# Last pass of a graph-attention and expert kernel: scalings three groups ahead, experts' pieces at the end of a step, and two late additions moved into the pass

## The chip, the cores and the metric

The kernel runs on one core of a Trainium2 chip. The metric is the device time of one execution in microseconds. Engines are named as in the profile: PE (TensorE), DVE (VectorE), ACT (ScalarE), POOL (GpSimd) and SP (SyncE, which here issues nearly all plain transfers). Each engine works through its own instructions in the order of the program.

## The reference

Input are 12500 nodes with 256 features and 212500 directed edges (self-loops included), sorted by target. First a graph attention layer with 4 heads adds its result to the nodes. Then a mixture of experts is applied to the new nodes x1. Cut to what matters here:

```python
x1 = x + gnn(layernorm(x))                       # attention over edges, bias, layernorm, relu
xn = layernorm(x1)
logits = mean(xn over all nodes) @ Wr + br       # ONE routing for all nodes
w, e = the two largest of the routing weights    # softmax of the two
y_k = gelu(xn @ W1[e_k] + b1[e_k]) @ W2[e_k] + b2[e_k]       # k = 0, 1
out = x1 + layernorm(w_0*y_0 + w_1*y_1 + xn, gamma, beta)
```

The routing needs the mean over all nodes, so it is known only when the last node has been through the attention layer. The last layernorm is taken over the feature axis of each node.

## The kernel before

**Tiles and groups.** The nodes are cut into 98 tiles of 128 rows (the last has 84), and the tiles into 25 groups of four (the last group, 24, has two tiles). The path of the code that these inputs take is `by_tiles` and then `weighted_sums`.

**The long loop** of `by_tiles` (L921 to L948) goes through 196 units of edges: POOL gathers rows, DVE and ACT make weights and messages, PE sums them for each tile. When a group's tiles are summed, a generator `nodes` (L398) is started for it. Each turn of the loop advances every running generator by one `yield`. `nodes` ends with three things: the statistics of x1 go to `stat` and PE adds the group's part of the mean to `pm` (L458); x1 is stored (L462); and one `yield` later DVE adds the vector beta to x1 (`xb`, L466), and that is stored as `x1b` (L469). The tile `xb` is in a pool with one buffer.

**The guess.** After group 0 the kernel guesses the two experts. It then runs the experts of a group in the shadow of the long loop (`experts`, L834): load xe, scale it on ACT (L841), transpose on PE (L850), copy (L855), eight hidden products with Gelu on ACT (L863, L868), and for each of the two experts two output products (L882), which DVE adds up (L886) and SP stores in `both` (L888). Between these are 12 `yield`s. The groups that are not begun by the end of the loop, the last three in the profile, are left to a generator `others` (L971), which starts a new chain each seven calls.

**After the loop** (L950 to L969) SP issues the loads of the first seven groups of the last pass (`final_loads`: two pieces of `both` and one of `x1b`, 512 KB each). The generators that still run are those of groups 23 and 24; they are driven to their end. Then the parts of the mean are added up (`sm`, L965), and `route` finds the real experts and their weights `ewc`. If the guess was right, the last pass follows.

**The last pass**, `weighted_sums` (L1290), goes through the 25 groups, one to a step. For each group it holds three slots out of seven of each kind: u and v (the results of the two experts, with the features on the partitions) and xb. For the first 16 groups (`MIXED`) ACT scales u by the first weight (L1306), DVE forms v times the second weight plus u (L1307), and PE transposes the result into PSUM (L1322). For the other groups PE does the weighing itself by two products with a weighted identity (L1325). DVE takes the statistics (L212, L213), ACT the root (L219), DVE the reciprocal and the offset (L220, L1339), ACT normalises in four instructions (L1343), and `stored` multiplies by gamma (L1352) and adds xb (L1354) into u's slot, which SP stores as output (L1356). The loads of group i + 7 into the slots of group i are issued last in step i. The tiles of PSUM are taken in turn from five buffers, two for a group.

The order within a step is written out by hand, and it is the order on each engine:

```python
        for i in range(NG):
            normed(i)
            weighed(i + 2)
            next(others, None)
            statistics(i + 1)
            transposed(i + 2)
            if i % 2:
                next(others, None)
            stored(i)
            held[i + SLOTS] = final_loads(take, i + SLOTS)
```

Of the kernel before, what the change touches and what calls it, by code (L numbers as in the profile page):

```python
# [37 lines left out]
F32 = mybir.dt.float32  # L38
# [8 lines left out]
P = 128  # L47
GN = 4
# [6 lines left out]
TOP_K = 2  # L55
# [4 lines left out]
def gnn_ffn_kernel(ctx: ExitStack, tc: tile.TileContext, x, src, dst, W, att_src, att_dst, bias,  # L60
                   g_gamma, g_beta, Wr, br, W1, b1, W2, b2, f_gamma, f_beta, out):
    nc = tc.nc
# [15 lines left out]
    def rows(t):  # L78
        return min(P, N - t * P)
# [318 lines left out]
    def nodes(pool, pm, a0, xc, ts, parts=((0, NT),), pool1=None):  # L398

        t0 = ts[0]
        den = pool.tile([P, GN, H], F32, name="den")
        for r, c0, c1 in spans(ts):
            av = a0[:r, c0:c1, :].rearrange("p t (h c) -> p t h c", h=H)
            nc.vector.tensor_scalar(den[:r, c0:c1, :], av[:, :, :, C], 1e-16, None, op0=ALU.add)
            nc.vector.reciprocal(den[:r, c0:c1, :], den[:r, c0:c1, :])
        yield
        o = (pool1 or pool).tile([P, GN, D], F32, name="o")
        ob = (pool1 or pool).tile([P, GN, D], F32, name="ob")  # L410
        for r, c0, c1 in spans(ts):
            n = c1 - c0
            av = a0[:r, c0:c1, :].rearrange("p t (h c) -> p t h c", h=H)
            nc.vector.tensor_tensor(
                o[:r, c0:c1, :].rearrange("p t (h c) -> p t h c", h=H), av[:, :, :, :C],
                den[:r, c0:c1, :, None].to_broadcast([r, n, H, C]), ALU.mult)
            nc.vector.tensor_add(ob[:r, c0:c1, :], o[:r, c0:c1, :],
                                 vec["bias"][:r, None, :].to_broadcast([r, n, D]))
        yield
        mv = pool.tile([P, GN, 2], F32, name="mvc")  # L420
        moments(pool, mv, ts, lambda j, r: ob[:r, j, :])
        yield
        rstd = pool.tile([P, GN], F32, name="rstdc")
        off = pool.tile([P, GN], F32, name="offc")
        inverse_std(pool, rstd, mv, ts)
        for r, c0, c1 in spans(ts):
            nc.vector.scalar_tensor_tensor(off[:r, c0:c1], mv[:r, c0:c1, 0], -1.0,
                                           rstd[:r, c0:c1], op0=ALU.mult, op1=ALU.mult)
        for j, t in enumerate(ts):
            r = rows(t)  # L430
            nc.scalar.activation(o[:r, j, :], ob[:r, j, :], AF.Identity, bias=off[:r, j:j + 1],
                                 scale=rstd[:r, j:j + 1])
        yield
        for r, c0, c1 in spans(ts):
            n = c1 - c0
            nc.vector.tensor_mul(ob[:r, c0:c1, :], o[:r, c0:c1, :],
                                 vec["gg"][:r, None, :].to_broadcast([r, n, D]))
            nc.vector.tensor_add(o[:r, c0:c1, :], ob[:r, c0:c1, :],
                                 vec["gb"][:r, None, :].to_broadcast([r, n, D]))
        yield  # L440
        mv2 = pool.tile([P, GN, 2], F32, name="mv2")
        for r, c0, c1 in spans(ts):
            nc.vector.scalar_tensor_tensor(  # L443
                xc[:r, c0:c1, :D], o[:r, c0:c1, :], 0.0, xc[:r, c0:c1, :D],
                op0=ALU.max, op1=ALU.add)
        moments(pool, mv2, ts, lambda j, r: xc[:r, j, :D])
        yield
        rstd2 = pool.tile([P, GN], F32, name="rstd2")
        inverse_std(pool, rstd2, mv2, ts)
        for r, c0, c1 in spans(ts):  # L450
            nc.vector.tensor_copy(stat[:r, t0 + c0:t0 + c1, 0], mv2[:r, c0:c1, 0])
            nc.vector.tensor_copy(stat[:r, t0 + c0:t0 + c1, 1], rstd2[:r, c0:c1])
            nc.vector.tensor_copy(xc[:r, c0:c1, D], mv2[:r, c0:c1, 0])
            nc.vector.scalar_tensor_tensor(stat[:r, t0 + c0:t0 + c1, 2], mv2[:r, c0:c1, 0], -1.0,  # L454
                                           rstd2[:r, c0:c1], op0=ALU.mult, op1=ALU.mult)
        for j, t in enumerate(ts):
            r = rows(t)
            nc.tensor.matmul(pm[-1], stat[:r, t, 1:2], xc[:r, j, :],  # L458
                             start=any(t == a for a, _ in parts),
                             stop=any(t == b - 1 for _, b in parts))  # L460
        for r, c0, c1, a in node_rows(x1, ts, D):
            nc.sync.dma_start(a, xc[:r, c0:c1, :D])  # L462
        yield
        xb = (pool1 or pool).tile([P, GN, D], F32, name="xb")
        for r, c0, c1 in spans(ts):
            nc.vector.tensor_add(xb[:r, c0:c1, :], xc[:r, c0:c1, :D],  # L466
                                 vec["fb"][:r, None, :].to_broadcast([r, c1 - c0, D]))
        for r, c0, c1, a in node_rows(x1b, ts, D):
            nc.sync.dma_start(a, xb[:r, c0:c1, :])  # L469
# [235 lines left out]
    def by_tiles():  # L705
# [4 lines left out]
        with tc.tile_pool(name="pe", bufs=1) as pe, \  # L710
# [194 lines left out]
            def forward(n):  # L905
# [8 lines left out]
                if (sought is not None and sought not in running and free_at <= n <= U - 12  # L914
# [2 lines left out]
                    running.append(experts(begun))  # L917
                    begun, free_at = begun + 1, n + EG

            waiting = set(range(len(groups)))  # L920
            for n in range(U + 2):  # L921
                if n + AH < U:
                    gather(units[n + AH])
                if n < U:
                    t, k0 = units[n]
                    if k0 == 0 and t % GN == 0:
                        group[t // GN] = node_tiles(pcw, groups[t // GN], table)
                    weights(units[n])
                if n + 1 < U:
                    targets(units[n + 1])  # L930
                if n < U:
                    edge_rows(units[n])
                if n + 2 < U:
                    across_rows(units[n + 2])
                if n < U:
                    messages(units[n])
                if 1 <= n <= U:
                    sums(units[n - 1])
                if n > 1 and units[n - 2][1] + UE >= TE:
                    t = units[n - 2][0]  # L940
                    node_sums(t)
                    g = t // GN
                    if t == groups[g][-1]:
                        a0, xc = group.pop(g)
                        with_nodes[g] = nodes(pcw, pm, a0, xc, groups[g], parts, pco)
                        running.append(with_nodes[g])
                        waiting.discard(g)
                forward(n)  # L948
            assert all(groups[g][0] >= LATE for g in with_nodes)
            sm = pe.tile([1, D + 1], F32, name="sm")  # L950
            nc.vector.tensor_add(sm, sm0, pm[-1])
            of_edges.close()
# [17 lines left out]

            def others():  # L971

                chains, g, n = [], begun, 0
                while chains or g < len(groups):
                    if g < len(groups) and n % EG == 0:
                        chains.append(experts(g))
                        g += 1
                    chains = further(chains)
                    n += 1
                    yield  # L980
# [309 lines left out]
    def weighted_sums(pe, take, psm, ahead, others):  # L1290
# [6 lines left out]
        for k in range(TOP_K):  # L1297
            nc.vector.tensor_scalar(by[:, k, :], ident, ewc[:, 2 * TOP_K + k:2 * TOP_K + k + 1],
                                    None, op0=ALU.mult)

        def weighed(i):

            if i < MIXED:
                n = sum(rows(t) for t in groups[i])
                u, v = (wide(piece)[:, :, :n] for piece in held[i][:2])
                nc.scalar.mul(u, u, ewc[:, 2 * TOP_K:2 * TOP_K + 1])  # L1306
                nc.vector.scalar_tensor_tensor(v, v, ewc[:, 2 * TOP_K + 1:], u,  # L1307
                                               op0=ALU.mult, op1=ALU.add)

# [36 lines left out]
        def stored(i):  # L1346
            s, _, xb = held.pop(i)
            p = ps.pop(i)
            for r, c0, c1 in spans(groups[i]):
                for c in range(c0, c1, 2):  # L1350
                    e = min(c + 2, c1)
                    nc.vector.tensor_mul(s[:r, c:e, :], p[c // 2][:r, c % 2:c % 2 + e - c, :],  # L1352
                                         vec["fg"][:r, None, :].to_broadcast([r, e - c, D]))
                nc.vector.tensor_add(s[:r, c0:c1, :], s[:r, c0:c1, :], xb[:r, c0:c1, :])  # L1354
            for r, c0, c1, a in node_rows(out, groups[i], D):
                nc.sync.dma_start(a, s[:r, c0:c1, :])  # L1356

        weighed(0)
        transposed(0)
        weighed(1)  # L1360
# [1 line left out]
        transposed(1)  # L1362
        for i in range(NG):
            normed(i)
            weighed(i + 2)
            next(others, None)
            statistics(i + 1)
            transposed(i + 2)
            if i % 2:
                next(others, None)  # L1370
            stored(i)
            held[i + SLOTS] = final_loads(take, i + SLOTS)


    ordered = nc.values_load(in_order, min_val=0, max_val=1)
    with tc.If(ordered != 0) as cmp:
# [31 lines left out]
```

## Time and profile before

| | |
|---|---|
| time, median of 3 runs | 2691.14 us (2683.43 to 2692.22) |
| the profiled execution: time, span | 2687.61 us, 2685.8 us |
| busy share of PE, DVE, ACT, POOL | 75%, 62%, 29%, 65% |
| last gather on POOL, and first step of the last pass (first L1343) | about 2407 us, 2475.35 us |
| last instruction of DVE in the last pass | ends at 2681.1 us |
| transfers over the whole span | 471.26 MB, mean 175 GB/s |

The shares are means over stages with quite different limits. In the last tenth POOL is at rest, so the last pass is read from its own stretch, 2411 to 2685.8 us.

### The profile page before, as it was taken

How to read it: one execution, taken by the hardware profiler on the slowest of the kernel's cores; microseconds unless marked ns; L12 is line 12 of the kernel's file. 1: busy time of each engine (PE TensorE's matmuls, PEld its weight loads, DVE VectorE, ACT ScalarE, POOL GpSimd, SP SyncE). 2: the span in 40 equal slices, each digit the busy share in tenths (PEclk: the TensorE clock that was granted, in tenths of full speed). 3: DMA queues.
4: the chain of work that ended last, by engine and by line, in shares of the span. 5: the costliest groups of instructions: out<-in, count | busy, mean ns of one | idle time of the engine just before them, and what ended most of it. 6: DMA issues, size and time to landing. Idle time of an engine off the chain costs nothing.

```text
span 2685.8 us, 25556 instructions
## 1 busy us (share of the span) xinstructions
PE 2004.4 (75%) x8326; PEld 1299.8 (48%) x8326; DVE 1670.0 (62%) x3149; ACT 788.5 (29%) x1283; POOL 1735.1 (65%) x1835
## 2 busy tenths in 40 slices
PE   6945555687878788878887788778778878872676
PEld 5734443454545555545554454455445544541336
DVE  7844655666565666566665666566666656665558
ACT  3410010232333223333223322322332233222554
POOL 1057777777777777777777777777777777760000
PEclk9977777899989999998889898988998888895788
DMA  7655456555655655665556556556555655545667
GB/s 208 211 162 151 131 165 195 154 171 181 186 144 178 184 175 163 189 180 164 169 179 179 156 180 178 163 158 188 175 161 170 180 179 161 174 123 202 210 216 224
DMA packets 248452, 471.26 MB, mean 175 GB/s; under 512 B 38348, under 2 KB 153800, under 8 KB 248114
## 3 DMA queue, kind: packets, MB, share of 16 engines
q0 software_dynamic: 84928, 240.36, 32.9%
q1 hardware_dynamic: 162566, 228.93, 25.5%
q8 instruction: 67, 1.10, 0.2%
q14 instruction: 75, 0.61, 0.1%
q10 hardware_dynamic: 816, 0.26, 0.0%
HBM read 391.75 MB, written 77.65 MB: 175 GB/s over the span
## 4 chain that ended last, share of the span: by engine, by line
POOL 44%; issue 23%; DVE 16%; DMA 7%; ACT 4%; PE 4%; SPq 1%; ACTq 0%; DVEq 0%; POOLq 0%; another core or an unknown queue 0%
POOL rows_w L729 44%; DMA rows_w<-table,src_c 6%; DVE ms L785 4%; DVE bn L212 3%; DVE oh L779 1%; ACT L772 1%; PE po_w L796 1%; PE ph_e L863 1%; ACT mix L1343 1%; DVE xc L443 1%; DVE whole L1354 1%; DVE ohT L743 1%; DVE whole L1352 1%; DVE y_e L886 1%; PE ph_e L882 1%
## 5 line engine op out<-in xcount | busy, mean ns | idle before, releaser
L729 POOL DMA_INDIRECT rows_w<-table,src_c x1764 | 1720.8, 975 | 539.7 <-issue 520.1
L796 PE MATMUL po_w<-ms,oh 128*128 128x260 f32 x3528 | 945.5, 429 | 2.4 <-DVE ms L785 2.4
L796 PEld LDWEIGHTS po_w<-ms,oh 128*128 128x128 f32 x3528 | 741.9, 215 | 131.8 <-DVE ms L785 3.2
L863 PE MATMUL ph_e<-xT_e,w1s 128*128 128x512 f32 (+1 forms) x800 | 420.5, 663 | 172.1 <-ACT hT_e L868 157.6
L785 DVE TENSOR_TENSOR ms<-rows_w,ad 128x2340 f32<-128x2340 f32 x196 | 506.2, 2583 | 0.0
L766 DVE TENSOR_TENSOR zw<-rows_w,adv 128x36 f32<-128x36 f32 x196 | 38.6, 197 | 637.5 <-DMA rows_w<-table,src_c 554.0
L779 DVE TENSOR_TENSOR oh<-jrow,ad 128x1152 f32<-128x1152 f32 x196 | 265.4, 1354 | 213.8 <-ACT ad L772 207.8
L882 PE MATMUL ph_e<-hT_e,w2s 128*128 128x512 f32 (+1 forms) x800 | 360.9, 595 | 18.3 <-ACT xT_e L855 18.3
L772 ACT ACT_TABLE_LOAD x113 | 145.0, 1283 | 772.5 <-DVE z3w L770 723.7
L863 PEld LDWEIGHTS ph_e<-xT_e,w1s 128*128 128x128 f32 x800 | 159.9, 210 | 365.8 <-ACT hT_e L868 205.9
L754 PE MATMUL ad<-t_all,ohT 128*128 128x25 bf16 x1764 | 77.5, 178 | 282.6 <-DVE ms L785 268.5
L772 ACT ACTIVATE ad<-z3w 128x36 f32<-128x36 f32 x196 | 40.0, 204 | 829.2 <-DVE z3w L770 764.4
L754 PEld LDWEIGHTS <-ohT 128*128 128x128 bf16 x1764 | 66.5, 99 | 404.9 <-DVE ms L785 344.1
L882 PEld LDWEIGHTS ph_e<-hT_e,w2s 128*128 128x128 f32 x800 | 154.0, 195 | 170.2 <-issue 144.2
L868 ACT ACTIVATE hT_e<-ph_e,b1c 128x512 f32<-128x512 f32 (+1 forms) x200 | 124.7, 673 | 13.2 <-PE ph_e L863 12.1
L868 ACT ACT_TABLE_LOAD x97 | 124.5, 1283 | 1.7
L743 DVE TENSOR_SCALAR ohT<-wb,pcol 128x1152 bf16<-128x1152 bf16 x196 | 102.6, 524 | 3.9 <-DMA srow<-in_src_dram,start_i 3.9
L458 PE MATMUL pm<-xc,stat 128*1 128x257 f32 x184 | 61.4, 493 | 51.6 <-DVE stat L454 43.0
L320 PE MATMUL ph<-WE,xT 128*128 128x264 f32 x392 | 96.7, 391 | 0.0
L333 POOL COPY tb<-ad_all 128x16 f32<-128x16 f32 (+2 forms) x26 | 5.1, 198 | 131.8 <-ACT ad_all L328 131.7
L320 PEld LDWEIGHTS ph<-WE,xT 128*128 128x128 f32 x392 | 71.7, 193 | 10.1
L219 ACT ACT_TABLE_LOAD x58 | 74.4, 1283 | 3.4 <-issue 2.4
(206 smaller groups left out, 1449.0 us busy)
## 6 DMA issues: line engine op xcount, KB each, us to landing
wb<-wrow_d SPq DMA_DIRECT2D x98, 576.0 KB
rows_w<-table,src_c POOLq DMA_INDIRECT x1764
both<-y_e SPq DMA_DIRECT2D x48, 512.0 KB
whole<-both SPq DMA_DIRECT2D x48, 512.0 KB
table<-tb SPq DMA_DIRECT2D x24, 528.0 KB
a<-table SPq DMA_DIRECT2D x24, 520.0 KB
xa<-in_x_dram SPq DMA_DIRECT2D x24, 512.0 KB
xc<-in_x_dram SPq DMA_DIRECT2D x24, 512.0 KB
```

Source lines behind the costliest of these rows:

```text
L212: nc.vector.bn_stats(bn[:r, j, :], get(j, r))
L320: nc.tensor.matmul(ph[:r, i, :HC + 2 * H], xT[:, i, d, :r], WE[:, d, :], start=(d == 0), stop=(d == KD - 1))
L729: nc.gpsimd.indirect_dma_start(out=got[u][:, k, :], out_offset=None, in_=table, in_offset=bass.IndirectOffsetOnAxis(ap=src_c[:, k0 + k, t: ...
L743: nc.vector.tensor_scalar(ohT[u], wb[t][:, k0 * P:(k0 + UE) * P], pcol, None, op0=ALU.is_equal)
L754: nc.tensor.matmul(ad[u][:, k * (6 * H + 1):(k + 1) * (6 * H + 1)], ohT[u][:, k * P:(k + 1) * P], t3_all[:, t, :], start=True, stop=True)
L772: nc.scalar.activation(ad[u][:, UW:].rearrange("p (k h) -> p k h", h=H), z3, AF.Exp)
L779: nc.vector.tensor_tensor(oh[u], jrow[:, None, :].to_broadcast([P, UE, P]), av[:, :, 6 * H:].to_broadcast([P, UE, P]), ALU.is_equal)
L785: nc.vector.tensor_tensor(ms[u].rearrange("p t (h c) -> p t h c", h=H), got.pop(u)[:, :, :MW].rearrange("p t (h c) -> p t h c", h=H), w[:, ...
L796: nc.tensor.matmul(po[t], e[:, k, :], m[:, k, :], start=(k0 + k == 0), stop=(k0 + k == TE - 1))
L863: nc.tensor.matmul(ph[m][:, :n], w1s[:, k, d, c * P:(c + 1) * P], xT[:, d, :n], start=(d == 0), stop=(d == KD - 1))
L868: nc.scalar.activation(hT[:, m, :n], ph.pop(m)[:, :n], AF.Gelu, bias=b1c[:, c, k:k + 1])
L882: nc.tensor.matmul(py[:, :n], w2s[:, k, c, d * P:(d + 1) * P], hT[:, k * KF + c, :n], start=(c == 0), stop=(c == KF - 1))
```

## The change

Three things are done. In `nodes`, groups from tile LATE on (the last two, 23 and 24) end after L462, without the addition of beta; the addition is put into a function of its own, `with_beta`, and `others` does it for these two groups at its first call, with two tiles of the pool that has one buffer of each name. In `weighted_sums` the scaling of u by ACT becomes a function of its own, `scaled`, which is called for three groups before the first step and in step i for group i + 3, while DVE's part stays at group i + 2. And the calls of `others` move: the one of each step to its end, behind `stored` and ahead of the loads, and the second one of odd steps from behind the transposes to ahead of them. In the new numbering of the file the lines behind the first edit are shifted.

```diff
@@ nodes
             nc.sync.dma_start(a, xc[:r, c0:c1, :D])
-        yield
-        xb = (pool1 or pool).tile([P, GN, D], F32, name="xb")
+        if t0 < parts[-1][0]:
+            yield
+            with_beta((pool1 or pool).tile([P, GN, D], F32, name="xb"), xc, ts)
+
+    def with_beta(xb, xc, ts):
+
         for r, c0, c1 in spans(ts):
             nc.vector.tensor_add(xb[:r, c0:c1, :], xc[:r, c0:c1, :D],
                                  vec["fb"][:r, None, :].to_broadcast([r, c1 - c0, D]))
@@ by_tiles
+            late = []
...
                         with_nodes[g] = nodes(pcw, pm, a0, xc, groups[g], parts, pco)
+                        if t >= LATE:
+                            late.append((xc, groups[g]))
...
             def others():
 
+                for name, (xc, ts) in zip(("xb", "ob"), late):
+                    with_beta(pco.tile([P, GN, D], F32, name=name), xc, ts)
                 chains, g, n = [], begun, 0
@@ weighted_sums
+        def scaled(i):
+
+            if i < MIXED:
+                n = sum(rows(t) for t in groups[i])
+                u = wide(held[i][0])[:, :, :n]
+                nc.scalar.mul(u, u, ewc[:, 2 * TOP_K:2 * TOP_K + 1])
+
         def weighed(i):
 
             if i < MIXED:
                 n = sum(rows(t) for t in groups[i])
                 u, v = (wide(piece)[:, :, :n] for piece in held[i][:2])
-                nc.scalar.mul(u, u, ewc[:, 2 * TOP_K:2 * TOP_K + 1])
                 nc.vector.scalar_tensor_tensor(v, v, ewc[:, 2 * TOP_K + 1:], u,
                                                op0=ALU.mult, op1=ALU.add)
...
+        for i in range(3):
+            scaled(i)
         weighed(0)
...
         for i in range(NG):
             normed(i)
+            scaled(i + 3)
             weighed(i + 2)
-            next(others, None)
             statistics(i + 1)
-            transposed(i + 2)
             if i % 2:
                 next(others, None)
+            transposed(i + 2)
             stored(i)
+            next(others, None)
             held[i + SLOTS] = final_loads(take, i + SLOTS)
```

More of the change, by code (lines that the diff above doesn't have):

```diff
@@ L948, in by_tiles @@
                 forward(n)
-            assert all(groups[g][0] >= LATE for g in with_nodes)
+            assert [groups[g][0] >= LATE for g in with_nodes] == [True, True]
             sm = pe.tile([1, D + 1], F32, name="sm")
```

## The prediction

> **What bounds the kernel now.** I read the page first (span 2685.8 us, profiled run 2687.61 us), then the chain of waits over the last 270 us, then the timelines of DVE, ACT and SP there, and last the stage windows. Up to about 2411 us the gathers of POOL set the pace and the diff touches nothing in that loop, so all that follows is about 2411 to 2685.8. Three things bound that stretch.
>
> First, the head. The chain, and the same place in the timeline of DVE (start, length, in brackets the idle time before it and who ended it):
>
> ```profile
> 2444.96 1.32 SPq L462
> 2446.38 10.09 DMA x1b<-xb
> 2456.49 0.76 DVE xb L466 x2
> 2458.00 1.02 PE mix L478 x4
> ```
>
> ```profile
> 2437.88 0.15 DVE L454 SCALAR_TENSOR_TENSOR stat<-mv,rstd 84x1 f32<-84x1 f32 x1
> 2456.49 0.76 DVE L466 TENSOR_TENSOR xb<-xc,v_fb 128x256 f32<-128x256 f32 x2 [18.46 <-DMA x1b<-xb]
> 2457.17 0.40 DVE L965 TENSOR_TENSOR sm<-sm,mix 1x257 f32<-1x257 f32 x1
> ```
>
> DVE stands idle for 18.46 us: the xb of the last group has one buffer, which the group before it is still storing, and that store was issued behind 21 loads. The sum for the routing (L965) needs no xb, it only stands behind it in DVE's order.
>
> Second, the steps of the last pass. One quiet step, DVE then ACT, and the two largest rows of the waits from 2457 on:
>
> ```profile
> 2484.58 0.16 DVE L1339 SCALAR_TENSOR_TENSOR offf<-mvf,rstdf 128x4 f32<-128x4 f32 x1
> 2488.06 1.28 DVE L1307 SCALAR_TENSOR_TENSOR whole<-whole,ewc 128x1024 f32<-128x1024 f32 x1 [3.33 <-ACT whole L1306]
> ...
> 2484.83 2.13 ACT L1343 ACTIVATE mix<-mix,offf,rstdf 128x256 f32<-128x256 f32 x4 [2.48 <-DVE offf L1339]
> 2486.89 1.14 ACT L1306 ACTIVATE whole<-whole,ewc 128x1024 f32<-128x1024 f32 x1
> ```
>
> ```profile
> DVE whole L1307 <- ACT whole L1306: 46.7, 15, 3.3
> ACT mix L1343 <- DVE offf L1339: 29.5, 18, 3.1
> ```
>
> DVE waits 3.3 us in each step for a scaling that ACT does only after the four normalisations of another group. A quiet step is 9.5 us (L1343 starts at 2475.35, 2484.83, 2494.32), of which DVE works 6.2.
>
> Third, a bound that hardly shows yet: the turn of SP's queue. The load of group i+7 into the first piece waits until the output of group i, which lies in that slot, has landed, and all that SP issues is in one order.
>
> ```profile
> 2484.52 0.38 SPq L1356 DMA_DIRECT2D out_dram<-whole  x1
> 2487.47 0.88 SPq L1283 DMA_DIRECT2D whole<-both  x2
> ...
> 2646.79 0.88 SPq L1283 DMA_DIRECT2D whole<-both  x2
> 2647.72 0.46 SPq L1162 DMA_DIRECT2D whole<-x1b  x1
> 2648.27 0.68 SPq L1356 DMA_DIRECT2D out_dram<-whole  x1
> 2656.12 0.87 SPq L1283 DMA_DIRECT2D whole<-both  x2
> ```
>
> With the transfers at rest a store holds SP for 2.95 us (2484.52 to 2487.47). Directly behind the three loads it holds it for 7.85, so that one turn (2646.79 to 2656.12) lasts 9.33 us, although the engines move no more than this (last two columns: DMA share, GB/s):
>
> ```profile
> 2425.00:2430.00 5.00, 0.00 (x0) 0.00 (x0) 4.76 (x16) 0.30 (x1) 0.00 (x0) 0.50 1.06 382
> 2646.50:2656.00 9.50, 7.62 (x64) 7.30 (x64) 9.10 (x25) 4.35 (x10) 0.00 (x0) 1.00 0.72 223
> ```
>
> **The change part by part.** *Residual plus beta of the last two groups leaves the nodes.* L466 of group 23 (1.19 us of DVE) and of group 24 (0.76) and three stores of L469 go. L965 then waits only for the four matmuls of L458, which end at 2437.76 + 1.64 = 2439.4; without the 1.19 us ahead of them, and with ACT as the partner in that stretch, I take 0.7 of it: 2438.7. Gain 2457.17 - 2438.7 = 18.5 us. What is late next is the route of 11 us from L965 to ewc, a chain of small DVE steps that I leave as it is; its bounds are 0 and 5 us longer, since it now runs while the loads still fill the transfers (share 1.07 until 2455); DVE's instructions at 2425 to 2437 show no stretching under the same load, so 0.
>
> The two adds come back inside the pass, behind the output of group 0: 1.19 + 0.76 = 2.0 us of DVE, once, and three stores on SP between output 0 and the loads of group 7. SP so waits for the adds and issues four DMAs (with the experts' xe load): the first load, T7, comes 4.0 us after DVE's end of step 0 instead of 3.0.
>
> *Scalings three groups ahead.* The same 16 instructions of L1306 (1.14 each), none added. Three stand ahead of the first step: the third ends some 3.3 us after ewc, while DVE's first two mixes and statistics take until 6 us after it (ACT idled 2.49 us there), so it is hidden. In step 0 the wait of 3.32 for the third mix is gone: DVE ends step 0 at 2484.46 - 18.5 - 3.3 = 2462.7, and T7 = 2466.7.
>
> In quiet steps DVE loses its 3.3: 6.3 us. In steps with an experts' Gelu ACT is the longer one: root 0.30, DVE's two small ones and the hops 0.5, four L1343 2.13, L1306 1.14, table load 1.28, two Gelus 1.26, table load 1.28 = 7.9 us (9.4 before). With two such calls in one odd step 1.26 more and about 1 for the matmul between them: 10 (11.1 before).
>
> *Experts' pieces at the end of a step.* A call issues the same xe loads, ACT, PE and DVE work and stores of both; on PE they now stand behind the transposes, on DVE and ACT behind stored, on SP still ahead of the loads of group i+7, but behind the output. POOL has nothing in the pass. The gain is small (transposes no longer behind 2 to 3 us of experts' matmuls, a delay that L1307's wait covered). The price: an xe load at the end of a step whose scaling stands in the middle of the next one. Before, ACT waited for such a load once (5.2 us, L841). Now that meets steps 1 and 5: about 3 and 8 us, 11 together; behind the waiting L841 on ACT stands the root of the next group, and DVE's reciprocal waits for that.
>
> Engines alone: steps 0 to 13 hold 6 quiet ones (38), 5 with one Gelu call (40), 3 with two (30), plus 11 = 118 us instead of 149.9 (2475.35 to 2625.25): 32 less. From step 14 on DVE takes 4.9 us a step as before.
>
> *The turn.* At 6.3 to 8 us a step DVE is faster than SP's turn of 9.33, so outputs are queued directly behind loads from step 1 on. Here the rule and the row part. The Trainium skill, page "DMA: Bandwidth & Descriptors", section on the anatomy of one DMA, gives about 2.0 us fixed, most of it the receipt of the write, plus the bytes at 436 GB/s. An isolated 512 KB store comes to 3.2 by it and 2.95 by the trace: agreed. For the turn (2.1 MB queued) it gives 2.0 + 4.8 = 6.8 us; then the turn would not bind and the engines' sum stands. The trace has 9.33 and, with the output 1.95 us behind the loads, 8.49 (2627.95 to 2636.44). The measurement decides: I take 9.2, nearer to the state that will hold.
>
> Experts' DMAs lengthen turns: with a 212 KB store of both they were 10.35 and 10.51, so 1.1 each; for 512 KB, scaled by 375 GB/s, 1.9 (an estimate from these rows). Five large ones and three small fall into the 17 turns from T7 to T24: 12.8 us. T24 = 2466.7 + 17 x 9.2 + 12.8 = 2635.9 (2666.63 before). Seven groups of lead let DVE run ahead until about step 21; then statistics of 23 and 24 wait for their loads. From T24: landing 2.7 (as before, 2669.3), 16 matmuls of L1325 1.9, statistics 1.1, output of 23 2.5, from there to the last DVE instruction 3.2, to the span's end 4.7: 16. Span 2652, time 2654 with the 1.8 us around the span. The profiled run was 2687.61, so 34 us less; the median shown, 2691.14, is 3.5 above that run, within the 9 us over which the three runs scatter, so I add nothing.
>
> **The rivals.** *The turn does not bind.* Then the end is 2681.1 - 18.5 - 3.3 - 32 = 2627.3, plus 2.0 for the moved adds and 4.7: span 2634, time 2636. For it: 375 GB/s were reached in the pure loads, and 8.49 was seen. Against: every turn after 2636 is over 9.
>
> *Only the head is gained.* Turns stay at the old mean, 179.2 / 17 = 10.5, because waits of ACT and PE on experts' pieces (15.2 and 15.7 us steps from 2524.28 and 2549.58) return in other places: 2466.7 + 179.2 + 16 = 2662, time 2664; with 5 us in the route and 5 in late xe loads up to 2674.
>
> *Slower.* The mechanism: each experts' DMA stands in SP between an output and the next loads and waits there for a late y_e, so that SP's turn grows until the loads arrive after DVE needs them. It decides when the mean turn passes 12.7 us: 2466.7 + 17 x 12.7 + 16 = 2698.6, time 2700. Turns of 13.0 and 15.3 have occurred (2537.07 to 2565.33), but only there, and a mean of 12.7 would need that in most of the 17.
>
> That the change does not do what it says would be: L965 still waiting for a store. Its inputs are sm and the sum in PSUM only, so I give it no more than the chance of no difference.
>
> **How the numbers follow.** Turn binds, 0.60: 2644 to 2660 (turn 8.7 to 9.7). Engines bind, 0.20: about 2636. Head only, 0.14: 2662 to 2674. No difference, 0.03; slower, 0.03. The time is that of the likeliest, 2654. The range reaches from the second case, with 3 us for scatter, to the top of the third: 2633 to 2674. A measurement of this kernel can tell about 0.3% (8 us) from no change; faster by more than that 0.94, within it 0.03, slower 0.03.
>
> **What would show it.** Right: L965 near 2439 with no long wait ahead of it; the row L1307 waiting for L1306 gone; quiet steps of 6.3 us; SP issuing outputs directly behind loads with turns of about 9 us; late in the pass, DVE's or PE's waits ending in the landing of whole<-both. Wrong: no wait for loads at the end (then 2636 is nearer), or ACT's waits for xe over 15 us in total, or turns above 10.5.

## The result, and the profile after

The changed kernel takes 2656.86 us (median of 4 runs, 2655.96 to 2661.83) against 2691.68 us before (4 runs): ratio 0.988, 95% interval 0.9857 to 0.9904. Its profiled execution has a span of 2654.2 us, 31.6 less than before. Line numbers behind the first edit have moved: L965 is now L972, L1306 is L1315, L1307 is L1322, L1339 is L1354, L1343 is L1358, L1352 is L1367, L1283 is L1292, L1356 is L1371, L841 is L845, L1325 is L1340.

The head, in the timeline of DVE (start, length, what ended the idle time before):

```profile
2437.74 0.14 DVE L454 SCALAR_TENSOR_TENSOR stat<-mv,rstd 84x1 f32<-84x1 f32 x1
2439.54 0.41 DVE L972 TENSOR_TENSOR sm<-sm,mix 1x257 f32<-1x257 f32 x1 [1.65 <-PE mix L458]
```

The wait of 18.46 us for a store is gone. What is left is 1.65 us for PE's last part of the mean; the sum of the means starts 17.6 us earlier than before (2457.17).

A quiet step (one without Gelu of the experts), DVE again:

```profile
2479.76 0.16 DVE L1354 SCALAR_TENSOR_TENSOR offf<-mvf,rstdf 128x4 f32<-128x4 f32 x1
2479.84 1.28 DVE L1322 SCALAR_TENSOR_TENSOR whole<-whole,ewc 128x1024 f32<-128x1024 f32 x1
```

The mix of u and v follows the offset without a gap; before it waited 3.33 us there. The step from L1358 at 2473.95 to that at 2479.96 is 6.0 us, before 9.5.

The queue of SP in the same stretch, and where it ends up:

```profile
2487.74 0.87 SPq L1292 DMA_DIRECT2D whole<-both  x2
2488.66 0.46 SPq L1171 DMA_DIRECT2D whole<-x1b  x1
2489.22 0.50 SPq L1371 DMA_DIRECT2D out_dram<-whole  x1
2496.81 0.87 SPq L1292 DMA_DIRECT2D whole<-both  x2
2497.73 0.46 SPq L1171 DMA_DIRECT2D whole<-x1b  x1
2498.28 0.66 SPq L1371 DMA_DIRECT2D out_dram<-whole  x1
2506.14 0.87 SPq L1292 DMA_DIRECT2D whole<-both  x2
2507.07 0.46 SPq L1171 DMA_DIRECT2D whole<-x1b  x1
2507.58 0.92 SPq L134 DMA_DIRECT2D xe<-x  x1
```

Here an output stands directly behind the loads, and the turn is 9.07 and 9.33 us. Before, such turns came only in the last 60 us; now they come in steps 2 to 5 and again from step 12 to the end. The last four lines also show the new stall: the xe load of the second chain comes behind loads that wait 7.9 us for an output. ACT, for which it was issued, stands still meanwhile, and DVE behind it:

```profile
2515.80 2.07 ACT L845 ACTIVATE xe<-xe,stat 128x256 f32<-128x256 f32 x4 [11.03 <-DMA xe<-x]
...
2519.51 0.18 DVE L220 RECIPROCAL rstdf<-std 128x4 f32<-128x4 f32 x1 [14.11 <-ACT std L219]
```

So in steps 6 to 11 it is SP that waits for DVE: the outputs come 2 to 9 us after SP is free, first here.

```profile
2518.04 0.46 SPq L1171 DMA_DIRECT2D whole<-x1b  x1
2525.73 0.38 SPq L1371 DMA_DIRECT2D out_dram<-whole  x1
```

The end, in the chain of waits:

```profile
2628.49 7.99 DMA out_dram<-whole
2636.53 0.36 SPq L1292
2636.99 2.99 DMA whole<-both
2640.03 2.57 PE mix L1340 x14
2642.62 0.44 DVE bn L212
```

An output holds SP for 8 us, then come the loads of the last group, PE waits for them and DVE for PE. From step 12 on every output is issued right behind its loads, with at most a store of y_e between, so DVE no longer keeps SP waiting: the end is set by the queue of SP. Steps 22 and 23 lose 6.5 us to it (9.5 and 6.4 us where before they took 4.9 and 4.5).

### The profile page after: what moved, and what is told of

Read it like the earlier page. It is cut to its first block, busy times and chain, and to the rows that moved or that the text cites. A ratio compares the mean times of both kernels' runs of the same rounds, so it can differ in the third digit from the quotient of the medians.

```text
span 2654.2 us, 25552 instructions
## 1 busy us (share of the span) xinstructions
PE 2008.5 (76%) x8326; PEld 1303.1 (49%) x8326; DVE 1671.9 (63%) x3149; ACT 788.8 (30%) x1283; POOL 1735.0 (65%) x1835
## 4 chain that ended last, share of the span: by engine, by line
POOL 43%; issue 23%; DVE 17%; DMA 8%; PE 5%; ACT 4%; ACTq 0%; DVEq 0%; SPq 0%; POOLq 0%; another core or an unknown queue 0%
POOL rows_w L733 43%; DMA rows_w<-table,src_c 6%; DVE ms L789 5%; DVE bn L212 2%; PE ph_e L867 2%; DVE oh L783 2%; PE po_w L800 1%; ACT L776 1%; DVE xc L443 1%; DVE ohT L747 1%; DVE y_e L890 1%; DMA out_dram<-whole 1%; PE ph_e L886 1%; DVE mv L213 1%; DVE whole L1367 1%
## 5 line engine op out<-in xcount | busy, mean ns | idle before, releaser
L867 PE MATMUL ph_e<-xT_e,w1s 128*128 128x512 f32 (+1 forms) x800 | 422.7, 666 | 155.4 <-ACT hT_e L872 145.1
L886 PE MATMUL ph_e<-hT_e,w2s 128*128 128x512 f32 (+1 forms) x800 | 354.0, 586 | 13.6 <-ACT xT_e L859 13.0
L867 PEld LDWEIGHTS ph_e<-xT_e,w1s 128*128 128x128 f32 x800 | 162.2, 212 | 349.8 <-ACT hT_e L872 191.5
L886 PEld LDWEIGHTS ph_e<-hT_e,w2s 128*128 128x128 f32 x800 | 151.1, 191 | 161.5 <-issue 139.6
```

The costliest lines, as they stand in the source:

```text
L867: nc.tensor.matmul(ph[m][:, :n], w1s[:, k, d, c * P:(c + 1) * P], xT[:, d, :n], start=(d == 0), stop=(d == KD - 1))
L886: nc.tensor.matmul(py[:, :n], w2s[:, k, c, d * P:(d + 1) * P], hT[:, k * KF + c, :n], start=(c == 0), stop=(c == KF - 1))
```

## The experiments

The theory: with the scalings out of DVE's way, the turn of SP's queue (loads, then an output that has to land before the next loads) sets the end of the pass. The rival: the steps of the engines set it (DVE's work, ACT with its table loads, PE with the experts' matmuls).

Four runs, marked "other chip" below, were on a chip on which the kernel before takes 3325 us (55 runs, granted clock 0.77 in place of 0.88); its long loop is slower there. Two of these kernels were run once more where before takes 2690 us. The pass itself hardly differs: from the start of the sum of the means to the end of the span it took 230.5 and 232.5 us for the one kernel, 216.3 and 217.6 for the other. This stretch, "the pass" from here on, is 228.6 us before and 214.7 after the change. All lengths of passes, steps and turns are of one profiled execution each.

**The head: a buffer, not the additions.** One name is changed in the kernel before; nothing is moved:

```diff
-        xb = (pool1 or pool).tile([P, GN, D], F32, name="xb")
+        xb = (pool1 or pool).tile([P, GN, D], F32, name="ob" if t0 == groups[-1][0] else "xb")
```

> The kernel before with one name changed: the sum with beta of group 24 goes into the tile ob, which is free by then, in place of xb; nothing is moved. Theory: the 18.46 us of DVE are a wait for that one buffer, so the sum of the means starts near 2440 and nearly the whole gain of the head is there: 16 to 18 us faster than before, time about 2673 to 2675. Rival, the additions themselves or their stores are what holds the head: less than 5 us faster.

2671.24 us, ratio 0.9938 (0.9925 to 0.995). Both additions stand where they stood, and DVE has no wait but that for PE:

```profile
2439.28 0.75 DVE L466 TENSOR_TENSOR ob<-xc,v_fb 128x256 f32<-128x256 f32 x2
2441.00 0.41 DVE L965 TENSOR_TENSOR sm<-sm,mix 1x257 f32<-1x257 f32 x1 [0.97 <-PE mix L458]
```

L466 is covered by PE's matmul (0.75 us of the 1.7 that L965 has to wait anyway). The pass is 228.1 us, as before. The 18.46 us were the wait for the one buffer.

**The head alone, as the change does it.** The additions go to `others`, the rest of the last pass is that of before (the hunks `nodes` and `by_tiles` of the change alone).

> The kernel with only the additions of beta moved, run once more where the kernel before takes about 2690 us: 16 to 18 us faster than before by the theory of the turn, time about 2672 to 2675; about 2657 if the head carries the whole gain.

2673.53 us, ratio 0.9937 (0.9925 to 0.9949). The sum of the means starts at 2438.55; the pass is 232.5 us, 3.9 longer than before. Of these, 1.8 us are the two additions, which now stand in its first step (11.3 us for 9.5); the rest is scattered over other steps, and on the other chip the pass is only 1.9 us longer than the 228.6. There:

> Only the additions of beta for groups 23 and 24 are moved into the pass; scalings and experts' calls stand as before. Theory of the turn: the sum of the means starts near 2439.5 as in the changed kernel (17.6 us earlier), the steps stay at 9.5 us and leave SP its idle time, so 16 to 18 us of the gain arrive at the end: time about 2671 to 2673. Rival, the head carries the whole gain: time about 2657. Rival, the head is given back later: about 2688.

3307.21 us, ratio 0.9949 (0.9934 to 0.9963), that is about 17 us. Moving the additions is not shown to gain more than the second buffer does.

**The scalings alone** (other chip): `scaled` with its calls at group i + 3 in the kernel before.

```diff
             normed(i)
+            scaled(i + 3)
             weighed(i + 2)
             next(others, None)
```

> Only the scalings stand three groups ahead; head and experts' calls as before. Theory of the turn: the first step loses 3.4 us, and from the loads of group 7 to those of group 24 it takes 169 us as in the changed kernel in place of 179, tail 17 to 18: 13 to 15 us less than before, time about 2674 to 2676. Rival, the engines set the end: six or more quiet steps lose 3.2 us each and those with a Gelu 1.5, 25 us or more less: time below 2668. Waits for L1306's scaling by DVE: 46.7 us before, below 5 here under both.

3312.87 us, ratio 0.9962 (0.9943 to 0.9981): 13 us, 6 to 19 by the interval. The pass is 214.7 us, 13.9 less than before, and from the loads of group 7 to those of group 24 it takes 169.6 us. The first quiet steps are 6.1 us, and steps 0 to 13 together take 129.2 us for 149.9, 20.7 less; a third of that does not reach the end. Head (17.6) and scalings (13.9) add up to the span's 31.6 us.

**The calls.** Alone, in the kernel before (other chip):

```diff
             weighed(i + 2)
-            next(others, None)
             statistics(i + 1)
-            transposed(i + 2)
             if i % 2:
                 next(others, None)
+            transposed(i + 2)
             stored(i)
+            next(others, None)
             held[i + SLOTS] = final_loads(take, i + SLOTS)
```

> Only the experts' calls are moved to the end of a step (the second one of odd steps ahead of the transposes); head and scalings as before. Theory: nothing that binds before is touched; the wait of ACT for the xe load of step 5 grows from 5.2 us to about 11, the transposes no longer behind experts' matmuls were covered by the wait for the scaling: 0 to 6 us slower than before, time 2691 to 2697. Rival, the calls carry part of the gain: 5 us or more faster, time below 2686.

3317.05 us, ratio 0.9981 (0.9963 to 0.9999): if anything faster, so my sign was wrong. The interval goes from 0.3 to 12 us and does not exclude the rival's 5; the pass is only 2.2 us shorter (226.4). The step with the xe load is 15.7 us against 15.2 before: with SP at rest between outputs, the load's later place costs half a microsecond and not six (ACT waits 5.8 us for it, before 5.2). And taken out of the changed kernel:

> The changed kernel with the experts' calls in their old places; head and scalings as changed. Theory of the turn: the 17 turns of SP set the end whatever the order of the calls, so within 3 us of the changed kernel (2654 to 2660), and waits for whole<-both at the end stay. Rival, steps of the engines set the end: the ACT wait for xe in step 5 goes from 11 us to about 5 and the kernel is 5 us or more faster (below 2652), or PE's late transposes cost 5 us or more (above 2662).

3292.39 us, ratio 0.9902 (0.9864 to 0.9941), 32 us by the ratio. The changed kernel itself has no run on that chip, so this cannot decide within 3 us. Once more, where before takes 2690 us:

> The changed kernel with the experts' calls in their old places, run once more where the kernel before takes about 2690 us: within 3 us of the changed kernel (2654 to 2660) by the theory of the turn; below 2652 or above 2662 if the place of the calls matters.

2661.53 us (2657.4 to 2663.04), ratio 0.9887 (0.9872 to 0.9901). The median is 1.5 us outside what I expected, but the interval overlaps that of the changed kernel; the passes are 216.3 and 217.6 us against 214.7. So the calls' new places are worth at most some 3 us in the pass, and the difference of 4.7 us in the medians cannot be told from none. The step with the xe load is 22 to 23.6 us with the calls in their old places too: the stall is not of the calls' making.

**The turn by itself.** The experts' work of the pass is left out:

```diff
-                while chains or g < len(groups):
+                while False:
...
         c0 = ts[0] * P
+        c0 = c0 if ts[0] < 22 * GN else 0
```

> The changed kernel without the experts of the last three groups (left out: their loads, products and stores; in their place the results of group 0 are read), so ACT, PE and DVE have no experts' work in the pass. Theory of the turn: 17 turns of 9.2 to 9.5 us from the loads of group 7 to those of group 24, so about 157 to 161 us, and 16 us behind: time about 2642 to 2648, with DVE waiting for loads in the second half in steps of 9 us. Rival, the engines set the end: steps of 6.3 us for groups 0 to 13 and 4.9 after, time about 2612.

2645.84 us (2644.15 to 2649.84). This is the sharpest of the runs: by my estimate from the steps of 6.3 and 4.9 us the engines alone would have ended near 2612. Behind the first step come nine of 6.1 us in a row; then steps 10 to 12 and 15 to 22 are stretched to 7.6 to 10.9 us. The queue of SP shows no work but its turn, and the waits of the pass name the loads as what holds the engines (us in total, times, longest; line numbers are one higher here):

```profile
2525.01 0.88 SPq L1293 DMA_DIRECT2D whole<-both  x2
2525.93 0.46 SPq L1171 DMA_DIRECT2D whole<-x1b  x1
2526.49 0.56 SPq L1372 DMA_DIRECT2D out_dram<-whole  x1
2534.37 0.88 SPq L1293 DMA_DIRECT2D whole<-both  x2
...
PE mix L1341 <- DMA whole<-both: 23.7, 17, 3.6
ACT whole L1316 <- DMA whole<-both: 18.1, 5, 5.7
```

One of ACT's five waits, 3.1 us, lies ahead of the first step and ends when the weights `ewc` are there; the other four, 15.0 us, are for loads. The 17 turns take 158.9 us, 9.35 each. The granted clock of TensorE was lower than in the changed kernel (0.50 for 0.81 in steps 0 to 13), but the turn was as long in the first ten steps, where DVE ran at 6.1 us, as later.

**The turn taken away.** The loads into the slots of group i - 1 are issued at the end of step i, when the output that they wait for has had a step to land. The lead is six groups in place of seven.

```diff
-            held[i + SLOTS] = final_loads(take, i + SLOTS)
+            if i:
+                held[i - 1 + SLOTS] = final_loads(take, i - 1 + SLOTS)
```

> The changed kernel, but the loads into the slots of group i-1 are issued at the end of step i in place of the end of step i-1, so that the output they wait for has had a step to land; the lead falls from seven groups to six. Theory of the turn: SP no longer waits 6 to 8 us for an output in each turn; turns follow DVE (6 to 8 us), the xe load of step 5 goes out earlier (ACT waits about 5 us or less for it in place of 11), the waits for whole<-both at the end (about 7 us) go: 10 to 20 us faster than the changed kernel, time 2637 to 2647. Rival, the engines' steps set the end: no more than 3 us faster, or slower because of the shorter lead.

2639.88 us, ratio 0.9816 (0.98 to 0.9833): 17 us below the changed kernel; of all kernels here this has the lowest time. The queue of SP, and ACT's wait for xe in the pass:

```profile
2503.01 0.38 SPq L1371 DMA_DIRECT2D out_dram<-whole  x1
2503.48 1.50 SPq L1292 DMA_DIRECT2D whole<-both  x2
2505.03 0.53 SPq L1171 DMA_DIRECT2D whole<-x1b  x1
...
ACT xe L845 <- DMA xe<-x: 4.5, 2, 2.4
```

Loads go out 0.47 us behind an output that is still under way, 17 turns take 136.4 us, no wait for whole<-both at the end is left, and the loads of the last group go out 30 us before the end in place of 17.7. The stall of the second chain fell with it: step 5 is 12.0 us in place of 20.9. So the turn had cost the pass (198.9 us for 214.7) in two places: about 9 us in steps 0 to 13, nearly all in step 5, and about 6 us of waits for the last loads.

**The stall for xe.** The second chain's load goes out at the first call, into a tile of its own:

```diff
+                early = {begun + 1: load_rows(pf, "xe_f", x1, groups[begun + 1], 1)}
                 chains, g, n = [], begun, 0
...
-                        chains.append(experts(g))
+                        chains.append(experts(g, early.get(g)))
```

> The changed kernel with the xe load of the second experts' chain (group 23) issued at the first call, into a tile of its own; nothing else. Theory of the turn: DVE's wait of 14.1 us in step 5 to 6 goes, but the turns of SP, still 9 to 9.5 us and longer with experts' stores, set the end: only the time that SP itself lay idle for it comes back, about 5 us (the load of group 13 went out 7 us after SP was free): 2 to 6 us faster than the changed kernel, and the waits for whole<-both at the end grow by about 8 to 10 us. Rival, the engines set the end: 11 to 14 us faster.

2651.22 us (2643.29 to 2652.9), ratio 0.9842 (0.9824 to 0.986): 5.6 us below the changed kernel by the medians, about 10 by the ratios, and the intervals overlap. So the times cannot tell my 2 to 6 us from the rival's 11 to 14. In the profile step 5 falls by 11 us, from 20.9 to 9.8, but step 1, whose xe load now shares SP's queue with the early one, grows by 2.5 (10.8 for 8.3); steps 0 to 13 together gain 8.6, and the pass 7.5 (207.2). The waits for the last loads did not grow by the 8 to 10 us that I expected: steps 21 and 22 lose 7.7 us to them, where the changed kernel loses 6.5. What the run does show is the turn: with the stall gone the outputs stand directly behind the loads from step 3 on, and the 17 turns take 161.5 us, 9.5 each, 7.6 less than in the changed kernel.

Both edits together:

> Both of the two edits before: loads a step later, and the second chain's xe load at the first call. Theory of the turn: with the turn gone the xe wait is worth what it shows: the steps of the engines set the end, 20 us or more faster than the changed kernel (time 2630 to 2637). Rival, engines alone set the end: equal to the kernel with the xe load alone.

2643.05 us, ratio 0.9824 (0.9808 to 0.9841). I had expected 2630 to 2637: a miss. The pass is 199.7 us against 198.9 without the early load. Step 5 gains 2.2 us, and step 1, whose own xe load now stands with one more transfer, loses 2.1 (10.4 against 8.3). There was no longer a long stall to take away, since the later loads had ended it already.

**The calls without the turn.** Loads a step later, calls in the old places:

> The kernel with the loads a step later, and the experts' calls in their old places (head and scalings as changed). Theory: without the turn the steps of the engines set the end; the old places save the wait for xe in step 1 (about 2 us) and cost a little in odd steps: within 3 us of the kernel with the loads a step later (2637 to 2643). Rival, the move of the calls is worth something once the turn is gone, since the transposes stand behind 2 to 3 us of experts' matmuls in some ten steps and the wait for the scaling no longer covers that: 8 us or more slower (above 2648).

2641.73 us, ratio 0.9819 (0.9806 to 0.9832); the pass is 199.5 us. Equal: the move of the calls is worth nothing measurable without the turn either.

## Why the prediction was right or wrong, point by point

- **The head**, 18.5 us: 17.6 in the profile, and 17.2 and 19.5 us alone in two kernels. Right, and the buffer as its cause is shown. The 0.7 us that I took for the removed addition is there (L454 of group 23 stands 0.67 us later in this run, 2430.93 for 2430.26, and PE's last part still starts at 2437.62 for 2437.76), but these matmuls ran 0.23 us longer.
- **First step**, 3.3 us: DVE ends step 0 at 2463.5, 24.0 us behind the sum, before 27.3. Right. T7 was forecast at 2466.7 and is 2467.47.
- **T24** (the loads of group 24) **and the end**: 2635.9 forecast, 2636.53 measured; 16 us behind it forecast, 17.7 measured; span 2652 forecast, 2654.2 measured. That the turn takes over is shown twice: by the run without experts, which ended at 2645.84 and not near 2612 although the engines had nothing else to do, and by the loads a step later, which took 17 us away. That T24 came out within 1 us is luck, as the next point shows. (For turns of 8.7 and 9.7 us my sum gives 2645 and 2662; I wrote 2644 and 2660.)
- **The terms under T24** were not all right; two errors cancel. I had 17 x 9.2 for the turns and 12.8 for the experts' DMAs, 169.2 together, and measured is 169.1. The runs split it otherwise, within a few us, as each is one profile: 158.9 for the bare turns (9.35 each); 161.5 with the experts' DMAs but one (the early xe load) and without the stall, so these DMAs cost some 3 us and not 12.8; and 7.6 for the stall for xe in step 5, while SP waited for DVE (it was free at 2518.5, and the next output came at 2525.73). The mis-sized term is the lengthening per experts' DMA. I took it from two turns of before (10.35 and 10.51) in which the store of y_e stood ahead of the output; the change puts four of the six behind it. In the changed kernel a turn with such a store of 512 KB behind the output took 9.17 us, one with 212 KB ahead of it 10.49:

```profile
2579.47 0.87 SPq L1292 DMA_DIRECT2D whole<-both  x2
2580.39 0.46 SPq L1171 DMA_DIRECT2D whole<-x1b  x1
2580.96 0.48 SPq L1371 DMA_DIRECT2D out_dram<-whole  x1
2581.53 0.50 SPq L892 DMA_DIRECT2D both<-y_e  x1
2588.64 0.87 SPq L1292 DMA_DIRECT2D whole<-both  x2
...
2626.05 0.87 SPq L1292 DMA_DIRECT2D whole<-both  x2
2626.97 0.46 SPq L1171 DMA_DIRECT2D whole<-x1b  x1
2627.53 0.87 SPq L892 DMA_DIRECT2D both<-y_e  x1
2628.49 0.42 SPq L1371 DMA_DIRECT2D out_dram<-whole  x1
2636.53 0.88 SPq L1292 DMA_DIRECT2D whole<-both  x2
```

That the place makes the difference is not tested alone. In the run with the early load the turns with such a store behind the output took 8.8 to 10.4 us, those with it ahead 9.5 and 9.9. The other error is the stall for xe, which I had only in the sum of the engines, as something that the lead would cover.

- **The engines' sum for steps 0 to 13**, 118 us forecast, 130.9 measured. Quiet steps and those with a Gelu are right (6.0 to 7.3; 7.3 to 7.8; 11.2, 10.0 and 8.2 for two calls). Step 5 was put at 16 and is 20.9, with an xe wait of 11.0 for my 8. Step 7 was put at 7.9 and is 14.5: its Gelu waits for hidden products that stand on PE behind the output products of the chain before (L867 at 2534.80, Gelu at 2536.72). Before, that step was the one of 15.7 us, which I had in hand and did not carry over. I expected that the lead would hide such delays from the end. For step 5 it did not: some 7 to 8 us of the stall reached the end, as the run with the early load shows. Step 7 was as long there (14.7), and the outputs still stood directly behind the loads, so with the stall gone its length is hidden.
- **The rule against the row.** The trace of before said 9.33 us for the turn, the run without experts 9.35. The Trainium skill, page "DMA: Bandwidth & Descriptors", section on the anatomy of one DMA, has 2.0 us plus the bytes at 436 GB/s, by which I estimated 6.8 for the turn and 2636 for the end; that fit is for one DMA issued from GpSimd, and here SP queues four. Choosing the measured row was the decisive step.
- **The rivals.** The turn does not bind: refuted for this kernel, and near to the truth once the turn is removed (2639.88 against the 2636 that it forecast). Head only: refuted, the scalings bring 13.9 us. Slower: the mean turn was 9.94 us, far from 12.7.
- **The calls.** I costed them as a small gain with a price in xe waits. The price exists, but most of it comes from SP's queue: the stall in step 5 is there with the calls in their old places too, and it shrinks to a wait of about 2 us when the loads no longer wait for the output just issued. Only the wait in step 1 comes from the calls' place: that step takes 8.3 us with them at the end and 6.1 in the old places.

What stays open: whether the calls' places are worth the 3 us at most that the passes suggest; and what makes the turn 9.35 us where its bytes would take 5.6 at the rate of the pure loads. That the output's landing closes the turn is shown. Of one turn of the run without experts (2525.01 to 2534.37), taken in slices of 0.5 us, nothing moved in the first microsecond after the issue and in the last 0.4; 4 us ran at 50 to 240 GB/s, at the start, in the middle and at the end, and 4 us at 300 to 410. What holds the rate down in the slow slices is not shown.

## What to carry to other kernels

Before you cut a wait on the engine that seems to bind, work out the period of every loop that runs beside it, above all a queue in which one instruction waits for the landing of the one before: here it took over at once and kept about half of what the engines could gain in the pass (15.8 of 29.7 us). Such a turn goes when the wait is issued a step later, at the price of one slot of lead. And when a long wait names a buffer, try a second buffer first: one changed name brought as much here as moving the work.

## What the runs showed of the hardware

A 512 KB output lands in about 2.9 us with the transfers at rest and in 7.9 directly behind 1.5 MB of loads, and a turn of both moves its 2.1 MB at about 225 GB/s, while the transfers queued ahead of the pass, without such a wait, ran at 370 to 382 GB/s for 30 us. On the chip that granted TensorE a mean clock of 0.77 in place of 0.88 the kernel before took 24% longer (3325 against 2691 us). In the kernel with the head alone, profiled on both, one gather took the same there (974 and 976 ns), but POOL stood idle before its gathers for 1146 us in place of 540, 609 of them until DVE's messages were done, and PE had 43% of the chain that ended last, where here POOL had 45%. That the clock is the cause is not shown. The last pass of one and the same kernel took 230.5 us there and 232.5 here: the clock in its steps 0 to 13 was 0.78 on both.
